# A new beginning of the first image and a new end of the last one, in a kernel that joins a Fourier neural operator and a 3x3 dilation

## The chip, the core and the metric

The kernel runs on one core of one Trainium2 chip. The metric is the device time of one execution in microseconds, and the median over several executions is what counts. Before the change it is 3658.42 us, the median of three executions that took 3650.33, 3659.02 and 3658.42 us.

A core has four compute engines that run side by side, each through its own list of instructions in order. TensorE (PE) multiplies matrices into an accumulator memory (PSUM); VectorE (DVE) does elementwise arithmetic, reductions, transposes and statistics; ScalarE (ACT) applies functions with a scale and a bias; GpSimd (POOL) is used here only to start transfers and for some constants. SyncE (SP) starts most transfers between the device's memory and the on-chip memory (SBUF). Engines wait for one another and for transfers through semaphores.

## The reference

The input x has 8 images of 8 channels of 256x256 pixels in float32. Two layers follow, each of them added to its own input.

```python
x = x + fno(gn(x))        # gn: mean and variance over each group of two channels
x = x + dilate(gn(x))     # 3x3 maximum, padded with -2

# fno, with 4 groups of 10 channels each
h = conv1x1([x, gridx, gridy], fc0)
for i in range(4):
    h = irfft2(modes_24x12(rfft2(h)) * sp_w[i]) + conv1x1(h, w_w[i])
    if i < 3: h = h * sigmoid(h * softplus(beta[i])) / 1.1
h = conv1x1(h, fc1)       # 10 to 128 channels in each group
h = h * sigmoid(h * softplus(beta[3])) / 1.1
return conv1x1(h, fc2)
```

The arithmetic on constants that matters here: softplus of the betas is multiplied into the weights (fc0 and w_w of layer 0, fc1), so that the activation becomes a plain Silu, and 1/(1.1 softplus) into the weights that follow. The group norm needs 1/sqrt(variance + eps).

## The kernel before

**Images and stages.** The eight images run one after another. For an image b, the four spectral layers run over eleven chunks of the state `h` (TensorE multiplies, ScalarE applies Silu, VectorE transposes for the next transform). After layer 3 the state goes to the device's memory, and the head (fc1, Silu, fc2, the sum with x, the dilation) of image b is worked off in small pieces between the steps of image b+1's layers. The order on TensorE, VectorE, ScalarE and SP is the order in which the program emits instructions (`tc.manual_schedule`); generators that `yield` let the main loop put pieces of one part between pieces of another.

**The beginning.** The program first emits loads: SP's queue gets the image (`load_x`, two halves of 1 MB, into `turned`), then `grp`, `fw`, `fw8`, `stack`, `er`, `unf`, `xe`, `wext` (lines 91 to 105), and GpSimd's queue the betas and the other constants. A transfer takes one of eight semaphores in turn, so the ninth transfer of a queue waits until the first has landed, the tenth for the second, and so on. Then come the constants' arithmetic: `softplus` (lines 139 to 153) for `beta_p` and `beta_a`, the factors `io`, the scaled fc1 and fc2 weights `w1` and `w2` (163 to 165), the products `p_wc` of fc0 and layer 0's weights on TensorE (171 to 175), `wc`, `wm`, `cv`, `cz` (176 to 198), and the scaled `wt` and `wext` (199 to 205). Lines 141 to 205 are emitted outside the hand-written order; in the profile they are found between the instructions of the first image's `start`.

**The first image.** `start(0, d)` (line 686) loads the first mode tables `t` and runs `spectrum_x`: eight `bn_stats` over the image (281), four `bn_aggr` (285), group means by TensorE (270, 272), variances, again group means, `rsqrt` (258), the normalisation of the image in four pieces (306), and then a chain of small transforms that alternates between TensorE (318, 324, 331, 343) and VectorE copies (319, 325, 334, 347). Products with `wext` (355) and a sum follow, then `mix` with the mode tables (420, 423), and `rows_even`, whose matmuls (496) and copies to `zt` (215, 217) precede the first burst of layer 0 (600, 606). For the later images the same generator is advanced inside the previous image's layer 3. Before the change, the main loop runs `start(0, d)` from end to end (941).

**rsqrt.** The start value comes from the integer form of the number, and four Newton steps of three dependent operations each follow (262 to 265). It is called once for each image's input and once for each image's output.

**The end of the last image.** Its output stays on chip in `ya` (16 rows of each of 128 stripes and one neighbour row above and below). Whenever two rows are complete, `add` calls `dilate_early(t)` (733): the maximum over three columns of these rows (`across`, into `ma`) and over three rows of those that have both neighbours (`down`, into `oa`). At t = 7 a transfer brings the last row of each stripe to row 0 of the next one (744). Then `dilate_last` runs `stats_end` (statistics of the image through two matmuls with `grp`, then `rsqrt`), finishes row 0 of the stripes (751 to 753), subtracts the mean and multiplies by 1/sigma (754), applies the padding values at the image's borders (756, 758), adds `ya` in four pieces of four rows (762) and sends each piece to the device's memory, from SP and GpSimd in turn (763).

Of the kernel before, what the change touches and what calls it, by code (L numbers as in the profile page):

```python
# [10 lines left out]
F32 = mybir.dt.float32  # L11
# [35 lines left out]
def fno_dilate_kernel(ctx: ExitStack, tc: tile.TileContext, a: dict, out: bass.AP):  # L47
# [14 lines left out]
    def ps_tri(name):  # L62
        return ps.tile([128, 3, 512], F32, tag="tri", bufs=2, name=name)
# [41 lines left out]
    nc.sync.dma_start(wext.rearrange("p g o j -> p (g o j)"), a["wext"].partition_broadcast(128))  # L105
# [30 lines left out]

    def softplus(t, n, name):
        e = const.tile([128, n], F32, tag=f"{name}_e", name=f"{name}_e")  # L140
        nc.vector.tensor_scalar(e, t, -1.0, None, ALU.mult)
        nc.vector.tensor_tensor(e, e, t, ALU.max)
        nc.scalar.activation(e, e, AF.Exp, scale=-1.0)
        nc.vector.tensor_scalar(e, e, 1.0, None, ALU.add)
        nc.scalar.activation(e, e, AF.Ln)
        sp = const.tile([128, n], F32, tag=f"{name}_sp", name=f"{name}_sp")
        nc.vector.tensor_scalar(sp, t, 0.0, None, ALU.max)
        nc.vector.tensor_tensor(sp, sp, e, ALU.add)
        nc.vector.tensor_scalar(sp, sp, 1e-20, None, ALU.max)
        rs = const.tile([128, n], F32, tag=f"{name}_rs", name=f"{name}_rs")  # L150
        nc.vector.tensor_scalar(rs, sp, 1.1, None, ALU.mult)
        nc.vector.reciprocal(rs, rs)
        return sp, rs

    sp_p, rs_p = softplus(beta_p, 4, "bp")
    sp_a, rs_a = softplus(beta_a, 4 * G, "ba")
    io = const.tile([128, 4 * G], F32, tag="io", name="io")
    nc.vector.tensor_copy(io[:, 0:4], sp_a[:, 0:4])  # L160
    nc.vector.tensor_tensor(io[:, 4:12], sp_a[:, 4:12], rs_a[:, 0:8], ALU.mult)
    nc.vector.tensor_copy(io[:, 12:16], rs_a[:, 8:12])
    nc.vector.tensor_scalar(w1, w1, sp_p[:, 3:4], None, ALU.mult)
    for g in range(G):
        nc.vector.tensor_scalar(w2[:, g, :], w2[:, g, :], rs_a[:, 12 + g : 13 + g], None, ALU.mult)


    wc = const.tile([128, 32], F32, tag="wc", name="wc")
    p = ps_tri("p_wc")
    for g in range(G):  # L170
        mm(p[32 * g : 32 * g + 6, 0, :32], fc0x[part(g), :], wt[part(g), 0, g, :], start=True, stop=True)
    for i in range(2):
        for r in range(4):
            mm(p[part(r), 1, NO * G * i : NO * G * (i + 1)], fc0c[:, i, :], wbd[:, NO * r : NO * (r + 1), :],
               start=True, stop=True)
    nc.vector.memset(wc, 0.0)
    for g in range(G):
        gs = slice(32 * g, 32 * g + 6)
        nc.vector.tensor_scalar(wc[gs, :], p[gs, 0, :32], sp_p[gs, 0:1], None, ALU.mult)

    wm = wbd
    nc.vector.memset(wm, 0.0)
    for g in range(G):
        nc.vector.tensor_scalar(wm[32 * g : 32 * g + 2, :WID, g], wc[32 * g : 32 * g + 2, :WID], -1.0, None, ALU.mult)
    cv = const.tile([128, 2, NO, G], F32, tag="cv", name="cv")
    nc.vector.tensor_tensor(
        cv.rearrange("p i o g -> p (i o) g"), p[:, 1, : 2 * NO * G].rearrange("p (i g) -> p i g", g=G),
        sp_a[:, 0:4].unsqueeze(1).to_broadcast([128, 2 * NO, G]), ALU.mult,
    )


    for i, l in enumerate((0, 2)):
        nc.vector.tensor_tensor(
            cz[:, i], cz[:, i], sp_a[:, 4 * l : 4 * l + 4].unsqueeze(1).to_broadcast([128, NO, G]), ALU.mult,
        )
    nc.vector.tensor_tensor(cz[:, 0], cz[:, 0], cv[:, 0], ALU.add)
    nc.vector.tensor_copy(cz[:, 2], cv[:, 1])
    nc.vector.tensor_scalar(cz1, cz1, sp_p[:, 1:2], None, ALU.mult)
    nc.vector.tensor_tensor(
        wt, wt, io.rearrange("p (l g) -> p l g", l=4).unsqueeze(3).to_broadcast([128, 4, G, 32]), ALU.mult,  # L200
    )
    nc.vector.tensor_tensor(
        wext.rearrange("p g o j -> p g (o j)"), wext.rearrange("p g o j -> p g (o j)"),
        io[:, 0:4].unsqueeze(2).to_broadcast([128, G, 5 * WID]), ALU.mult,
    )


    alone = [True]

# [523 lines left out]
    def dilate_early(t):  # L733

        across(1 + 2 * t, 3 + 2 * t)
        if t == 0:
            nc.gpsimd.dma_start(ya[0:127, 17, 1 : HW + 1], ya[1:128, 1, 1 : HW + 1])
        else:
            down(2 * t - 1, 2 * t + 1)
        if t == 3:  # L740
            nc.vector.tensor_scalar(ya[:, 17, :], ya[:, 17, :], edge[:, 1:2], None, ALU.min)
            across(17, 18)
        if t == 7:
            nc.gpsimd.dma_start(ya[1:128, 0, 1 : HW + 1], ya[0:127, 16, 1 : HW + 1])
            down(15, 16)

    def dilate_last(b, stats):
        d = {}
        yield from stats_end(stats, f"y{b}", d)
        mr = d["mr"]  # L750
        nc.vector.tensor_scalar(ya[:, 0, :], ya[:, 0, :], edge[:, 0:1], None, ALU.min)
        across(0, 1)
        down(0, 1)
        nc.vector.tensor_scalar(oa, oa, mr[:, 0:1], mr[:, 1:2], ALU.subtract, ALU.mult)
        for w in (0, HW - 1):
            nc.vector.tensor_scalar(oa[:, :, w : w + 1], oa[:, :, w : w + 1], PAD, None, ALU.max)
        for i, r in enumerate((0, 15)):
            nc.vector.tensor_scalar(oa[:, r, :], oa[:, r, :], edge[:, 2 + i : 3 + i], None, ALU.max)
        o_rows = out[b].rearrange("c (p r w) -> (c p) r w", p=16, r=16)
        for i in range(4):  # L760
            r = slice(4 * i, 4 * i + 4)
            nc.vector.tensor_tensor(oa[:, r], oa[:, r], ya[:, 4 * i + 1 : 4 * i + 5, 1 : HW + 1], ALU.add)
            (nc.sync, nc.gpsimd)[i % 2].dma_start(o_rows[:, r], oa[:, r])
        yield


# [22 lines left out]
    def head(b, stored, stats):  # L789
# [147 lines left out]

    stats_of = {}
    with tc.manual_schedule(engines={PE, DVE, ACT, SP}):
        d = {}  # L940
# [50 lines left out]
def _tables():  # L991
# [153 lines left out]
```

## Time and profile before

| what | value |
| --- | --- |
| median of three executions | 3658.42 us |
| the profiled execution | 3659.15 us |
| its span, from the first to the last instruction | 3657.4 us |
| TensorE busy | 3478.5 us, 95% |
| ScalarE busy | 2873.7 us, 79% |
| VectorE busy | 2381.7 us, 65% |
| first burst of layer 0 begins (L600) | 58.37 us |
| last add of the last image ends (L851) | 3631.87 us |
| last VectorE operation ends (L762) | 3651.53 us |

A line of the page or of an answer reads: line of the program, engine, operation, tile written<-tiles read, shape, count, and times. In a timeline the first two numbers are the start and the length in us, and square brackets give the idle time of the engine just before and what ended it. A view by waits gives who waited for whom: us in total, times, longest. "SPq" and "POOLq" are the queues of the engines that start transfers. The two spans of the program that the change touches are the first 60 us and the last 26 us; in the page's 40 slices of the span, TensorE is busy for nine tenths or more of each slice from the fifth to the last but one.

### The profile page before, as it was taken

The page shows a single profiled execution, that of the slowest core. Times are in us where ns is not written, and L with a number is a line of the kernel's source. Part 1 is how long each engine was busy: PE and PEld are TensorE (multiplying, and loading weights), DVE is VectorE, ACT ScalarE, POOL GpSimd, SP SyncE. Part 2 cuts the span into 40 slices and gives each one's busy share as a digit, 9 for nine tenths or more (in the row PEclk, how much of TensorE's full clock was granted, in tenths as well). Part 3 has the DMA queues.
Part 4 walks back from the last instruction along what each step waited for, and adds up shares of the span by engine and source line. Part 5 has one row for each costly group of instructions (what it writes and reads, how often), then busy time and mean ns, then how long its engine had stood idle before and what let it go on. Part 6 is the DMA issues. An engine that isn't in the chain of part 4 may idle for free.

```text
span 3657.4 us, 112630 instructions
## 1 busy us (share of the span) xinstructions
PE 3478.5 (95%) x50872; PEld 1271.2 (35%) x50872; DVE 2381.7 (65%) x3697; ACT 2873.7 (79%) x3035; POOL 117.0 (3%) x202
## 2 busy tenths in 40 slices
PE   5768999999999999999999999999999999999997
PEld 2323333333333333333333333333333333333222
DVE  6776656557775677756776577766777567772443
ACT  2435888888888888887888888888888888889986
POOL 1000000000000000000000000000000000000000
PEclk7878999999999999999999999999999999999998
DMA  3005211442225222271223512254222521225331
GB/s 93 16 15 206 58 47 50 152 121 65 76 87 185 81 60 73 87 226 55 64 60 126 183 56 76 64 166 119 67 76 87 192 81 53 71 70 191 83 84 48
DMA packets 114080, 344.70 MB, mean 94 GB/s; under 512 B 15985, under 2 KB 18481, under 8 KB 98177
## 3 DMA queue, kind: packets, MB, share of 16 engines
q1 hardware_dynamic: 95392, 276.32, 24.9%
q0 software_dynamic: 18208, 61.18, 5.3%
q8 instruction: 400, 6.55, 0.7%
q14 instruction: 80, 0.65, 0.1%
HBM read 213.44 MB, written 123.74 MB: 92 GB/s over the span
## 4 chain that ended last, share of the span: by engine, by line
PE 80%; DVE 13%; ACT 4%; issue 3%; DMA 0%; ACTq 0%; DVEq 0%; POOL 0%; POOLq 0%
PE p_fc L825 21%; PE p_fc L842 21%; PE p_z L606 10%; PE p_d L567 8%; PE p_z L603 8%; PE p_u L585 3%; PE p_z L600 3%; DVE y L851 2%; DVE S L423 2%; DVE turned L420 2%; DVE turned L550 2%; PE p_b L390 1%; DVE turned L381 1%; PE p_g L518 1%; ACT act L826 1%
## 5 line engine op out<-in xcount | busy, mean ns | idle before, releaser
L827 ACT ACTIVATE act<-p_fc 128x1536 f32<-128x1536 f32 x1024 | 1492.0, 1457 | 3.1 <-PE p_fc L825 3.1
L825 PE MATMUL p_fc<-hs,c_w 32*128 32x512 f32 x8192 | 1132.7, 625 | 24.6 <-DVE y L851 10.0
L842 PE MATMUL p_fc<-act,c_w 128*32 128x512 f32 x8192 | 1007.1, 599 | 0.5 <-ACT act L827 0.2
L826 ACT ACTIVATE act<-p_fc 128x512 f32<-128x512 f32 x1024 | 616.0, 602 | 199.7 <-PE p_fc L825 187.6
L550 DVE STREAM_TRANSPOSE turned<-h 128x1024 f32<-128x1024 f32 x528 | 632.6, 1226 | 196.0 <-ACT h L611 195.2
L611 ACT ACTIVATE h<-p_z 128x512 f32<-128x512 f32 (+1 forms) x528 | 512.0, 1021 | 205.8 <-PE p_z L606 205.8
L851 DVE TENSOR_TENSOR y<-p_fc,y 128x512 f32<-128x512 f32 x392 | 267.7, 683 | 526.0 <-PE p_fc L842 526.0
L825 PEld LDWEIGHTS p_fc<-hs,c_w 32*128 32x128 f32 x8192 | 357.9, 184 | 595.0 <-ACT act L826 260.2
L842 PEld LDWEIGHTS p_fc<-act,c_w 128*32 128x32 f32 x8192 | 222.4, 109 | 704.9 <-issue 327.4
L606 PE MATMUL p_z<-c_binv,zt 32*128 32x256 f32 x5632 | 414.2, 408 | 0.1
L606 PEld LDWEIGHTS p_z<-c_binv,zt 32*128 32x128 f32 x5632 | 261.2, 188 | 309.5 <-issue 296.1
L603 PE MATMUL p_z<-h,c_wt 32*32 32x512 f32 x8448 | 358.0, 601 | 7.9 <-ACT act L826 4.2
L567 PE MATMUL p_d<-turned,c_fw 32*32 32x480 f32 (+1 forms) x9216 | 308.0, 539 | 0.6 <-DVE turned L550 0.2
L575 ACT ACTIVATE turned<-p_d 128x1440 f32<-128x1440 f32 x144 | 183.1, 1272 | 89.7 <-PE p_d L567 86.6
L613 ACT ACTIVATE h<-p_z,c_bias 128x512 f32<-128x512 f32 (+1 forms) x176 | 186.6, 1111 | 72.0 <-PE p_z L606 71.8
L215 ACT ACTIVATE zt<-p_g 128x198 f32<-128x198 f32 (+2 forms) x132 | 62.5, 583 | 177.6 <-PE p_g L496 93.7
L423 DVE TENSOR_REDUCE S<-turned 128x80 f32<-128x800 f32 x192 | 188.9, 984 | 5.9
L420 DVE TENSOR_TENSOR turned<-t,B 128x800 f32<-128x800 f32 x192 | 188.7, 983 | 1.1
L567 PEld LDWEIGHTS p_d<-turned,c_fw 32*32 32x32 f32 x9216 | 127.5, 103 | 165.5 <-issue 63.8
L381 DVE STREAM_TRANSPOSE turned<-zt 128x960 f32<-128x960 f32 x96 | 177.1, 1868 | 2.5
L603 PEld LDWEIGHTS p_z<-h,c_wt 32*32 32x32 f32 x8448 | 92.9, 103 | 175.5 <-DVE y L851 48.8
L585 PE MATMUL p_u<-turned,c_stack 128*32 128x480 f32 (+1 forms) x1152 | 136.7, 543 | 7.2 <-DVE turned L574 6.2
(198 smaller groups left out, 1748.2 us busy)
## 6 DMA issues: line engine op xcount, KB each, us to landing
stored<-h SPq DMA_DIRECT2D x88, 1024.0 KB
hs<-stored SPq DMA_DIRECT2D x352, 256.0 KB
t<-in_spw SPq DMA_DIRECT2D x96, 400.0 KB
yin<-y_rows POOLq DMA_DIRECT2D x56, 512.0 KB, 5.1
h<-in_xp SPq DMA_DIRECT2D x352, 48.0 KB
turned<-in_xw SPq DMA_DIRECT2D x16, 1024.0 KB
y<-in_x SPq DMA_DIRECT2D x56, 256.0 KB
y_rows<-y POOLq DMA_DIRECT2D x56, 256.0 KB, 3.9
```

The lines of the kernel that those rows point to most:

```text
L420: nc.vector.tensor_tensor(pr, sw[k], bt[:, k2, k].unsqueeze(2).to_broadcast([128, G, 2 * WID, WID]), ALU.mult)
L423: nc.vector.tensor_reduce(s[k2][:, k].rearrange("p s o g -> p (s o) g"), pr.rearrange("p g m i -> p m g i"), AX.X, ALU.add,)
L550: nc.vector.transpose(dst[:, 2 * i : 2 * i + 2], h[:, c, 2 * i : 2 * i + 2].rearrange("p f (s x) -> p f s x", s=2))
L567: mm(banks[q][part(v % 4), : 240 * n], fw8[part(q), v, :], t[part(q), :, :, v, : NBLK * WID], start=v < 4, stop=v >= 4)
L603: mm(o, wt[part(q), l, g, :], h[part(q), c, f, :], start=True, stop=False)
L606: mm(banks[q][:, HW * s : HW * (s + 1)], zt[part(q), 2 * c + s].rearrange("p f o -> p (f o)"), binv[part(q), :], start=False, stop=s == 1)
L611: nc.scalar.activation(dst, src, AF.Silu)
L825: mm(banks[g], w1[part(g), blk, :], hs[k][part(g), :], start=True, stop=True)
L826: nc.scalar.activation(act[:, 0, :], one, AF.Silu)
L827: nc.scalar.activation(act[:, 1:4, :], tri, AF.Silu)
L842: mm(acc[part(g), :], w2[:, g, 15 - rb - i : 47 - rb - i], act[:, g, :], start=i == 0, stop=i == 1)
L851: nc.vector.tensor_tensor(y, sums, y, ALU.add)
```

## The change

It has five parts.

1. SP's loads are put in another order: `er`, `fw`, `unf`, `xe` and `wext` follow the image, and `fw8`, `stack` and `grp` come last.
2. The arithmetic on the constants becomes a generator, `prepare()`, in eight pieces. The main loop emits a piece after the third, sixth, eighth, tenth, twelfth, fourteenth and sixteenth yield of `start(0, d)`, and the last piece after it.
3. `rsqrt` makes three Newton steps instead of four, for every image.
4. At the last image's t = 7 only the transfer of the neighbour rows is started; `dilate_early(7)` is no longer called, and `dilate_last` does its work itself.
5. `dilate_last` is rewritten. The statistics come first; the remaining `across` operations lie between their two matmuls. ScalarE takes the mean off `oa`, piece by piece (`centre`). The padding values are scaled by sigma instead of the rows by 1/sigma (`ends`), and one operation multiplies by 1/sigma and adds `ya`. Five pieces (rows 4 to 7, 8 to 11, 12 to 15, 0 and 1, 2 and 3) go out, all from SP. In the `edge` table the value for rows that are no border becomes -1e30, so that its product with sigma stays finite.

```diff
     ident = const.tile([128, 128], F32, tag="ident", name="ident")
     make_identity(nc, ident)
-    grp = load("grp", (128, 128), nc.sync)
-    fw = load("fw", (128, 2, 32), nc.sync)
-    fw8 = load("fw8", (128, 8, 32), nc.sync)
-    stack = load("stack", (128, 32), nc.sync)
...
     er = load("er", (128, 2, 32), nc.sync)
+    fw = load("fw", (128, 2, 32), nc.sync)
     unf = load("unf", (128, 3, 32), nc.sync)
...
     nc.sync.dma_start(wext.rearrange("p g o j -> p (g o j)"), a["wext"].partition_broadcast(128))
+    fw8 = load("fw8", (128, 8, 32), nc.sync)
+    stack = load("stack", (128, 32), nc.sync)
+    grp = load("grp", (128, 128), nc.sync)
...
+    def prepare():
...
+        for i, (t, _, _) in enumerate(pair):
+            nc.vector.tensor_scalar(e[i], t, -1.0, None, ALU.mult)
+            nc.vector.tensor_tensor(e[i], e[i], t, ALU.max)
+        for i in range(2):
+            nc.scalar.activation(e[i], e[i], AF.Exp, scale=-1.0)
+        yield
+        for i, (t, _, _) in enumerate(pair):
+            nc.vector.tensor_scalar(e[i], e[i], 1.0, None, ALU.add)
+            nc.vector.tensor_scalar(sp[i], t, 0.0, None, ALU.max)
+        for i in range(2):
+            nc.scalar.activation(e[i], e[i], AF.Ln)
+        yield
+        p = ps_tri("p_wc")
...
+        yield
+        for i in range(2):
+            nc.vector.tensor_tensor(sp[i], sp[i], e[i], ALU.add)
+            nc.vector.tensor_scalar(sp[i], sp[i], 1e-20, None, ALU.max)
+            nc.vector.tensor_scalar(rs[i], sp[i], 1.1, None, ALU.mult)
+            nc.vector.reciprocal(rs[i], rs[i])
...
+        yield
+        nc.vector.memset(wc, 0.0)
...
+        yield
+        nc.vector.tensor_tensor(
+            wt, wt, io.rearrange("p (l g) -> p l g", l=4).unsqueeze(3).to_broadcast([128, 4, G, 32]), ALU.mult,
+        )
+        nc.vector.tensor_scalar(w1, w1, sp_p[:, 3:4], None, ALU.mult)
+        for g in range(G):
+            nc.vector.tensor_scalar(w2[:, g, :], w2[:, g, :], rs_a[:, 12 + g : 13 + g], None, ALU.mult)
+        yield
...
-        for _ in range(4):
+        for _ in range(3):
...
-        if t == 7:
-            nc.gpsimd.dma_start(ya[1:128, 0, 1 : HW + 1], ya[0:127, 16, 1 : HW + 1])
-            down(15, 16)
 
     def dilate_last(b, stats):
...
+        nc.vector.bn_aggr(mv, stats.rearrange("p n s -> p (n s)"))
+        p = ps_tri("p_st_end")[:, 0, 0:1]
+        mm(p, grp, mv[:, 0:1], start=True, stop=True)
+        rows = ma[:, 15:17]
+        nc.vector.tensor_tensor(rows, ya[:, 15:17, 0:HW], ya[:, 15:17, 1 : HW + 1], ALU.max)
+        nc.vector.tensor_copy(m, p)
+        nc.vector.tensor_tensor(d, mv[:, 0:1], m, ALU.subtract)
+        nc.vector.scalar_tensor_tensor(mv[:, 1:2], d, d, mv[:, 1:2], ALU.mult, ALU.add)
+        q = ps_tri("p_sv_end")[:, 0, 0:1]
+        mm(q, grp, mv[:, 1:2], start=True, stop=True)
+        nc.vector.tensor_scalar(less, m, -1.0, None, ALU.mult)
+        nc.vector.tensor_tensor(rows, rows, ya[:, 15:17, 2 : HW + 2], ALU.max)
+        v = mv[:, 1:2]
+        nc.vector.tensor_scalar(v, q, EPS, None, ALU.add)
+        rsqrt(v, r, d)
+        nc.vector.tensor_tensor(d, v, r, ALU.mult)
+        nc.vector.tensor_scalar(ends[:, 1:2], d, -2.0 * PAD, None, ALU.mult)
+        nc.vector.tensor_scalar(ends[:, 2:4], edge[:, 2:4], d, -2.0, ALU.mult, ALU.mult)
+
+        def centre(r0, r1):
+            nc.scalar.activation(oa[:, r0:r1], oa[:, r0:r1], AF.Identity, bias=less)
+
+        centre(4, 8)
+        centre(8, 12)
+        centre(1, 4)
+        centre(12, 13)
+        down(13, 15)
+        centre(13, 15)
+        down(15, 16)
+        centre(15, 16)
         nc.vector.tensor_scalar(ya[:, 0, :], ya[:, 0, :], edge[:, 0:1], None, ALU.min)
         across(0, 1)
         down(0, 1)
-        nc.vector.tensor_scalar(oa, oa, mr[:, 0:1], mr[:, 1:2], ALU.subtract, ALU.mult)
...
+        centre(0, 1)
         o_rows = out[b].rearrange("c (p r w) -> (c p) r w", p=16, r=16)
-        for i in range(4):
-            r = slice(4 * i, 4 * i + 4)
-            nc.vector.tensor_tensor(oa[:, r], oa[:, r], ya[:, 4 * i + 1 : 4 * i + 5, 1 : HW + 1], ALU.add)
-            (nc.sync, nc.gpsimd)[i % 2].dma_start(o_rows[:, r], oa[:, r])
+        for r0, r1 in ((4, 8), (8, 12), (12, 16), (0, 2), (2, 4)):
+            o = oa[:, r0:r1]
+            side = o[:, :, 0 : HW : HW - 1]
+            nc.vector.tensor_scalar(side, side, ends[:, 1:2], None, ALU.max)
+            for i, row in enumerate((0, 15)):
+                if r0 <= row < r1:
+                    nc.vector.tensor_scalar(oa[:, row, :], oa[:, row, :], ends[:, 2 + i : 3 + i], None, ALU.max)
+            nc.vector.scalar_tensor_tensor(o, o, r, ya[:, r0 + 1 : r1 + 1, 1 : HW + 1], ALU.mult, ALU.add)
+            nc.sync.dma_start(o_rows[:, r0:r1], o)
         yield
...
-                dilate_early(t)
+                if t < 7:
+                    dilate_early(t)
+                else:
+                    nc.gpsimd.dma_start(ya[1:128, 0, 1 : HW + 1], ya[0:127, 16, 1 : HW + 1])
...
-        d = {}
-        for _ in start(0, d):
-            pass
+        d, ready = {}, prepare()
+        for n, _ in enumerate(start(0, d), 1):
+            if n in (3, 6, 8, 10, 12, 14, 16):
+                next(ready)
+        next(ready)
...
-    edge[:, 2], edge[:, 3] = np.where(top, PAD, -BIG), np.where(bottom, PAD, -BIG)
+    edge[:, 2], edge[:, 3] = np.where(top, PAD, -1e30), np.where(bottom, PAD, -1e30)
```

The pieces of `prepare()` that the cut leaves out are the same operations as before: the twelve `p_wc` matmuls, `io` and the scaled `wext` behind the reciprocals, the four `wc` operations, `cv` with the memset and the four operations of `wm`, and `cz`. As built, the order on VectorE begins with the eight `bn_stats` and the four `bn_aggr`; on TensorE the `p_wc` matmuls stay between the second group means and L318; `wt`, `w1` and `w2` come between the last operation on `fz` and the first `zt` copy.

More of the change, by code (lines that the diff above doesn't have):

```diff
@@ L135, in fno_dilate_kernel @@
     nc.vector.memset(dc, 0.0)
[L139 to L153, printed above, removed]
@@ L157, in fno_dilate_kernel @@
-    sp_p, rs_p = softplus(beta_p, 4, "bp")
-    sp_a, rs_a = softplus(beta_a, 4 * G, "ba")
-    io = const.tile([128, 4 * G], F32, tag="io", name="io")
[L160 to L165, printed above, removed]
@@ L168, in fno_dilate_kernel @@
-    wc = const.tile([128, 32], F32, tag="wc", name="wc")
[L169 to L179, printed above, removed]
+    io = const.tile([128, 4 * G], F32, tag="io", name="io")
@@ L181, in fno_dilate_kernel @@
+    wc = const.tile([128, 32], F32, tag="wc", name="wc")
     wm = wbd
-    nc.vector.memset(wm, 0.0)
-    for g in range(G):
-        nc.vector.tensor_scalar(wm[32 * g : 32 * g + 2, :WID, g], wc[32 * g : 32 * g + 2, :WID], -1.0, None, ALU.mult)
     cv = const.tile([128, 2, NO, G], F32, tag="cv", name="cv")
[L186 to L189, printed above, removed]
@@ L192, in fno_dilate_kernel @@
-    for i, l in enumerate((0, 2)):
+    def prepare():
+        pair = ((beta_p, 4, "bp"), (beta_a, 4 * G, "ba"))
+        e, sp, rs = [[const.tile([128, n], F32, tag=f"{name}_{k}", name=f"{name}_{k}") for _, n, name in pair]
+                     for k in ("e", "sp", "rs")]
+        for i, (t, _, _) in enumerate(pair):
[12 more added lines that the diff above has]
+        for g in range(G):
+            mm(p[32 * g : 32 * g + 6, 0, :32], fc0x[part(g), :], wt[part(g), 0, g, :], start=True, stop=True)
+        for i in range(2):
+            for r in range(4):
+                mm(p[part(r), 1, NO * G * i : NO * G * (i + 1)], fc0c[:, i, :], wbd[:, NO * r : NO * (r + 1), :],
+                   start=True, stop=True)
+        yield
+        for i in range(2):
+            nc.vector.tensor_tensor(sp[i], sp[i], e[i], ALU.add)
+            nc.vector.tensor_scalar(sp[i], sp[i], 1e-20, None, ALU.max)
+            nc.vector.tensor_scalar(rs[i], sp[i], 1.1, None, ALU.mult)
+            nc.vector.reciprocal(rs[i], rs[i])
+        (sp_p, sp_a), (_, rs_a) = sp, rs
+        nc.vector.tensor_copy(io[:, 0:4], sp_a[:, 0:4])
+        nc.vector.tensor_tensor(io[:, 4:12], sp_a[:, 4:12], rs_a[:, 0:8], ALU.mult)
+        nc.vector.tensor_copy(io[:, 12:16], rs_a[:, 8:12])
@@ L193, in fno_dilate_kernel @@
         nc.vector.tensor_tensor(
-            cz[:, i], cz[:, i], sp_a[:, 4 * l : 4 * l + 4].unsqueeze(1).to_broadcast([128, NO, G]), ALU.mult,
-        )
[L196 to L205, printed above, removed]
+            wext.rearrange("p g o j -> p g (o j)"), wext.rearrange("p g o j -> p g (o j)"),
@@ new lines, in prepare @@
+            io[:, 0:4].unsqueeze(2).to_broadcast([128, G, 5 * WID]), ALU.mult,
+        )
+        yield
+        nc.vector.memset(wc, 0.0)
+        for g in range(G):
+            gs = slice(32 * g, 32 * g + 6)
+            nc.vector.tensor_scalar(wc[gs, :], p[gs, 0, :32], sp_p[gs, 0:1], None, ALU.mult)
+        yield
+        nc.vector.tensor_tensor(
+            cv.rearrange("p i o g -> p (i o) g"), p[:, 1, : 2 * NO * G].rearrange("p (i g) -> p i g", g=G),
+            sp_a[:, 0:4].unsqueeze(1).to_broadcast([128, 2 * NO, G]), ALU.mult,
+        )
@@ new lines, in prepare @@
+        nc.vector.memset(wm, 0.0)
+        for g in range(G):
+            gs = slice(32 * g, 32 * g + 2)
+            nc.vector.tensor_scalar(wm[gs, :WID, g], wc[gs, :WID], -1.0, None, ALU.mult)
+        yield
+        for i, l in enumerate((0, 2)):
+            nc.vector.tensor_tensor(
+                cz[:, i], cz[:, i], sp_a[:, 4 * l : 4 * l + 4].unsqueeze(1).to_broadcast([128, NO, G]), ALU.mult,
+            )
+        nc.vector.tensor_tensor(cz[:, 0], cz[:, 0], cv[:, 0], ALU.add)
+        nc.vector.tensor_copy(cz[:, 2], cv[:, 1])
@@ L208, in fno_dilate_kernel @@
+        nc.vector.tensor_scalar(cz1, cz1, sp_p[:, 1:2], None, ALU.mult)
+        yield
+        nc.vector.tensor_tensor(
+            wt, wt, io.rearrange("p (l g) -> p l g", l=4).unsqueeze(3).to_broadcast([128, 4, G, 32]), ALU.mult,
+        )
+        nc.vector.tensor_scalar(w1, w1, sp_p[:, 3:4], None, ALU.mult)
+        for g in range(G):
+            nc.vector.tensor_scalar(w2[:, g, :], w2[:, g, :], rs_a[:, 12 + g : 13 + g], None, ALU.mult)
+        yield
     alone = [True]
@@ L742, in dilate_early @@
             across(17, 18)
-        if t == 7:
-            nc.gpsimd.dma_start(ya[1:128, 0, 1 : HW + 1], ya[0:127, 16, 1 : HW + 1])
-            down(15, 16)
     def dilate_last(b, stats):
-        d = {}
-        yield from stats_end(stats, f"y{b}", d)
-        mr = d["mr"]
+        mv = sb.tile([128, 2], F32, tag="mv", name="mv_end")
+        mr = sb.tile([128, 2], F32, tag="mr", bufs=4, name="mr_end")
+        d = sb.tile([128, 1], F32, tag="d", name="d_end")
+        ends = sb.tile([128, 4], F32, tag="mv", name="ends")
+        m, r, less = mr[:, 0:1], mr[:, 1:2], ends[:, 0:1]
+        nc.vector.bn_aggr(mv, stats.rearrange("p n s -> p (n s)"))
[26 more added lines that the diff above has]
+        centre(15, 16)
         nc.vector.tensor_scalar(ya[:, 0, :], ya[:, 0, :], edge[:, 0:1], None, ALU.min)
@@ L753, in dilate_last @@
         down(0, 1)
[L754 to L758, printed above, removed]
-        o_rows = out[b].rearrange("c (p r w) -> (c p) r w", p=16, r=16)
-        for i in range(4):
-            r = slice(4 * i, 4 * i + 4)
-            nc.vector.tensor_tensor(oa[:, r], oa[:, r], ya[:, 4 * i + 1 : 4 * i + 5, 1 : HW + 1], ALU.add)
-            (nc.sync, nc.gpsimd)[i % 2].dma_start(o_rows[:, r], oa[:, r])
+        centre(0, 1)
+        o_rows = out[b].rearrange("c (p r w) -> (c p) r w", p=16, r=16)
+        for r0, r1 in ((4, 8), (8, 12), (12, 16), (0, 2), (2, 4)):
[7 more added lines that the diff above has]
+            nc.sync.dma_start(o_rows[:, r0:r1], o)
         yield
@@ L939, in fno_dilate_kernel @@
     with tc.manual_schedule(engines={PE, DVE, ACT, SP}):
-        d = {}
-        for _ in start(0, d):
-            pass
+        d, ready = {}, prepare()
[3 more added lines that the diff above has]
+        next(ready)
         for b in range(n_img):
```

## The prediction

> **What bounds the kernel now.** I read the page first, then the waits of the first 60 us, then the timeline of both ends, since the change touches only these and one helper (rsqrt).
>
> ```profile
> PE 3478.5 (95%) x50872; PEld 1271.2 (35%) x50872; DVE 2381.7 (65%) x3697; ACT 2873.7 (79%) x3035; POOL 117.0 (3%) x202
> PE 80%; DVE 13%; ACT 4%; issue 3%; DMA 0%; ACTq 0%; DVEq 0%; POOL 0%; POOLq 0%
> ```
>
> Over the span TensorE carries the chain that ended last (80%). That average hides both ends: before 58 us and after 3632 us TensorE works for a few us at a time, and VectorE, in program order, sets the pace. What stood in front of VectorE at the start is in the waits of 0 to 60 us (one for VectorE, one for SP's queue):
>
> ```profile
> DVE bp_e L141 <- DMA c_beta_p<-in_beta_p: 3.9, 1, 3.9
> SPq L105 <- DMA turned<-in_xw: 4.1, 1, 4.1
> ```
>
> VectorE waits first for the betas, then for softplus, although the image is there: SP's wait at L105 is for the image's second half, and the timeline has the next issue at 10.17, so that half landed by then; the same reading of the issue at 5.69 puts the first half at about 5.6. In the timeline, VectorE's statistics come only after that arithmetic:
>
> ```profile
> 10.17 0.33 SPq L105 DMA_DIRECT2D c_wext<-in_wext  x1
> 14.26 2.46 DVE L281 BATCH_NORM_STATS2 bn_x<-turned 128x6 f32<-128x512 f32 x4
> 16.64 0.41 DVE L285 BATCH_NORM_AGGREGATE mv_x<-bn_x 128x2 f32<-128x12 f32 x4
> 19.66 0.17 DVE L302 TENSOR_SCALAR d_x<-p_sv_x 128x5 f32<-128x5 f32 x1 [0.93 <-PE p_sv_x L272]
> 26.37 2.98 DVE L306 TENSOR_SCALAR turned<-turned,mr_x 128x1024 f32<-128x1024 f32 x4
> ```
>
> Everything after 26.37 up to the first row matmuls (54.67) hangs on this line. At the end, TensorE's last add is over at 3631.87, and then VectorE alone runs to 3651.53:
>
> ```profile
> 3636.14 0.58 DVE L231 BATCH_NORM_AGGREGATE mv_y<-h 128x2 f32<-128x96 f32 x1
> 3641.40 0.35 DVE L751 TENSOR_SCALAR h<-h,c_edge 128x258 f32<-128x258 f32 x1
> 3643.62 2.41 DVE L754 TENSOR_SCALAR h<-h,mr_y 128x4096 f32<-128x4096 f32 x1
> 3646.90 4.62 DVE L762 TENSOR_TENSOR h<-h 128x1024 f32<-128x1024 f32 x4
> ```
>
> The view by windows has the output's data until 3655.0 (near 400 GB/s, 1.3 us per 512 KB) and nothing more to the span's end at 3657.4: a tail of 2.4 us.
>
> **The start, step by step.** (1) The statistics move in front of everything that needs the betas. First four: 5.7 to 8.2, free. Second four: from 10.2, 2.46 as above; the aggregates add 0.41 less 0.08 overlap: they end at 13.0, not 17.05: **4.1 earlier**. (2) From there to L302 is 2.61 (17.05 to 19.66), two round trips to TensorE with 0.93 idle each. The betas' eight small operations (0.17, pitch 0.1 to 0.2) go into these two waits, about 0.6 and 0.45: cost 0. Exp, Ln and their table load (1.28) end on ScalarE by about 15.7, and the results are asked for at about 20.8. The twelve p_wc matmuls lie between two uses of TensorE (0.7 of over 2 us). L302 falls at 15.6. (3) L302 to L306 took 6.71, because wext, wt, wc, wm, cv, cz, w1 and w2 were mixed in. Image 1 shows it bare: L302 at 305.24, L306 at 308.11, 2.87 with four Newton steps; a step is three dependent operations, 0.20 apart. Three steps: 2.27. L306 begins at 17.9, **8.5 earlier**. (4) What was mixed in is paid later, in VectorE's waits: softplus' rest, io, wext and the memset (13 operations, about 2.4 from their pitches) in 2.60 idle before L319: 0. wc (0.09 and 1.02) in 0.81 before L325: +0.35. cv, wm (1.0) in 1.16 before L334: 0. cz (0.65) in 0.62 before L347: +0.05. wt, w1, w2 (0.68, 0.41, 0.70) in 1.42 before the first zt copy L217: +0.37, which the first bursts inherit since TensorE waits for zt at 60.3. Start: 8.5 - 0.77 = **7.7**.
>
> The reordered SP loads: er, fw, unf, xe, wext, fw8 (400 KB) now follow the image instead of 380 KB, and wext no longer waits; the mode tables t start some 0.7 us sooner and h's 44 loads behind them too. grp, now last before t, is first needed by image 0's output statistics. Nothing waits that did not. If the image's second half landed later by d, d is lost; I take 0, and 0 to 3 as ends, 3 being about what 1.2 MB of t would take.
>
> **The Newton step in images 1 to 7** (x and y, 0.6 each): 0. After L306's first piece VectorE idles anyway (near 1147: 0.99 until TensorE's p_fc); after the y chain at 816.5 it idles 0.80 for ScalarE. At image 1 the fourth L306 piece paces one matmul of L318 by perhaps 0.1. Ends: 0 to -1.
>
> **The end.** From 3631.87: bn_stats to 3632.67. The aggregate comes at once, to 3633.27, instead of after L725 to L731 (3.5). TensorE's answer 0.68 later, the chain L239 to L252 1.35: 3635.3. Two across operations (0.69 each) fit into those two waits (0.68, 0.74): +0.1. rsqrt with three steps 2.73 - 0.58 = 2.15, three new small ones 0.5: 3638.0. Then what was moved behind: down(13,15) 1.43, down(15,16) 0.86, and row 0 as before (L751 to L731, 2.2): 3642.5, against 3643.62. The real gain follows: L754 (2.41) leaves VectorE. ScalarE takes the mean off rows 1 to 12 from 3634.6: by L613, an Identity with a pointer bias (688 ns at 512, 1533 at 1536), pieces of 1024, 1024, 768, 256 cost 1.11, 1.11, 0.90, 0.48, done at 3638.2; rows 13 to 15 and 0 follow each down. The last ends near 3643 and is asked for at 3647; cover 4 us. Five side maxima (0.17, 0.19 with their wait) 0.95, two edge rows 0.62, and 4096 elements of a three-operand operation.
>
> That one has no row at this size. [...] L754 (0.59 ns an element) beside L762 (1.19) shows it, so fusing multiply and add makes nothing faster than L762; only moving the subtraction to ScalarE pays. Next rows: L762 1.216 (1.13 pitch) per 1024; L849, this operation from PSUM at 512, 747 against 693. Ends 1.13 and 1.31; I take 1.2, and 0.67 for 512: 4.94 in all (-0.3, +0.5).
>
> VectorE ends at 3642.5 + 6.5 = 3649.0. Pieces are ready at 3643.9, 3645.3, 3647.0, 3648.15, 3649.0; SP's first transfer before took 0.8 from issue (3648.14) to data. The data never queue more than 0.2: the last 256 KB run 3649.8 to 3650.45; plus 2.4: 3652.85 against 3657.4: **4.55**. All issues now sit on SP, which has nothing else left; POOL's two go.
>
> **Sum.** 7.7 + 4.55 = 12.25. The profiled execution is 3659.15 (span 3657.4), so 3646.9; the median of the runs shown is 0.7 lower: **3646**, 0.34% down.
>
> **The clock.** TensorE is slow in the first image:
>
> ```profile
> 58.00:62.00 4.00, 4.00 (x51) 1.53 (x48) 0.67 (x1) 2.42 (x3) 0.00 (x0) 0.50 0.02 4
> 70.00:74.00 4.00, 4.00 (x52) 1.54 (x48) 2.37 (x3) 1.94 (x2) 0.00 (x0) 0.50 0.00 0
> 76.00:78.00 2.00, 2.00 (x64) 0.88 (x61) 0.86 (x2) 1.21 (x2) 0.00 (x0) 1.00 0.00 0
> ```
>
> (window; us, busy of PE, PEld, DVE, ACT, POOL; clock; DMA.) [...] busy all of 58 to 74 at 0.50, and full only a good microsecond into the first transform (74.33). [...] by the row the slow stretch moves along with the work and costs what it did. I take the row. [...]
>
> **Rivals.** *The clock rises early* in the first image: 3646 - 5.4 = 3640.5. For it: one of the three runs was at 3650.33, 8 under the others. Against: this profile. *The start gives less*: the image's half lands up to 3 later or the small operations overrun their waits by 1 to 2: 3649 to 3650. For it: eight extra waits on ScalarE, TensorE and loads in that stretch, two covers with under 0.2 to spare; against: every result is ready microseconds early. *The change moves nothing at the start* (the image, not the betas, was late): only the end, 3654; against: the issue at 10.17. *Slower*: moved by 7.7, the first transforms do not lift the clock, and layer 0 of image 0 goes on at 0.50. In 78 to 107 TensorE is busy some 28 us; at half clock that costs up to 25: 3671. It decides once the slow stretch lasts some 25 us longer than now. For it: 16 busy us did not lift it; against: transforms lifted it within 1.2 us.
>
> **How the numbers follow.** Forecast (3643 to 3649) 0.60; early clock 0.14; less start 0.19; end only 0.04; slower 0.03. The range 3638 to 3652 takes in the first three, the unknown ends and part of the runs' spread. 0.3%, about what a measurement of this kernel can tell from none, is 11 us: 3647.4. Three quarters of the forecast case, the early clock and little of the third are under it: 0.64 faster; slower 0.03; same 0.33.
>
> **What would show it.** In the new trace: the second statistics at about 10.2, L306's line at about 18, the first row matmuls near 47; aggregate near 0.8 us after the last add, ScalarE idle before row 0's piece, last VectorE operation 17.1 after the last add, tail 2.4. Wrong would be: idle time for a DMA before the second statistics, waits of TensorE for the constants, the three-operand operation over 1.3, or a first full clock elsewhere than at the first transform.

## The result, and the profile after

The changed kernel takes 3642.47 us, the median of five executions (3640.12 to 3646.95); the kernel before, run beside it, 3659.02 (3650.33 to 3661.19). The ratio is 0.996, with a 95% interval of 0.9949 to 0.9972. The forecast was 3646, a gain of 12.25; the medians are 16.55 apart, the spans of the two profiled executions (3657.4 and 3640.6) 16.8.

Shares and chain in the page of the changed kernel have hardly moved:

```profile
PE 3475.6 (95%) x50872; PEld 1269.6 (35%) x50872; DVE 2374.1 (65%) x3656; ACT 2878.2 (79%) x3042; POOL 115.9 (3%) x200
PE 79%; DVE 13%; ACT 4%; issue 3%; DMA 1%; SPq 0%; DVEq 0%; ACTq 0%
```

VectorE has 41 operations less, TensorE as many as before. The timeline of the changed kernel's start (start, length, engine, line, operation, tiles) answers to the lines from 14.26 on:

```profile
10.00 2.47 DVE L286 BATCH_NORM_STATS2 bn_x<-turned 128x6 f32<-128x512 f32 x4 [1.86 <-DMA turned<-in_xw]
12.39 0.41 DVE L290 BATCH_NORM_AGGREGATE mv_x<-bn_x 128x2 f32<-128x12 f32 x4
15.41 0.16 DVE L307 TENSOR_SCALAR d_x<-p_sv_x 128x5 f32<-128x5 f32 x1 [0.63 <-PE p_sv_x L277]
17.68 2.98 DVE L311 TENSOR_SCALAR turned<-turned,mr_x 128x1024 f32<-128x1024 f32 x4
```

The statistics now wait for the image, and the normalisation (L311, was L306) begins 8.69 earlier. The end, from the aggregate to ScalarE's work, the first fused operation and the last:

```profile
3621.10 0.59 DVE L756 BATCH_NORM_AGGREGATE mv_end<-h 128x2 f32<-128x96 f32 x1
3622.87 3.41 ACT L776 ACTIVATE h<-h,ends 128x1024 f32<-128x1024 f32 x4 [4.46 <-DVE ends L766]
3630.58 1.29 DVE L798 SCALAR_TENSOR_TENSOR h<-h,mr_end 128x1024 f32<-128x1024 f32 x1
3636.68 0.75 DVE L798 SCALAR_TENSOR_TENSOR h<-h,mr_end 128x512 f32<-128x512 f32 x1
```

From the start of the last add (3631.18 before, 3619.59 after) to the end of the span it is 21.01 us instead of 26.17: 5.2 gained. That leaves 11.6 at the last add. The starts of the same instructions in both traces, before less after, say where they arose:

| instruction, time before | gain |
| --- | --- |
| first row matmuls, 54.67 | 8.6 |
| image 1, variance (L302), 305.24 | 6.2 |
| image 1, add at 343.2 | 7.1 |
| image 2, add at 784.1, then at 794.8 | 7.16, then 8.70 |
| image 3, adds at 1217.6 and 1228.2 | 8.73, then 10.26 |
| image 4, adds at 1651.1 and 1661.7 | 10.36, then 11.89 |
| image 5, adds at 2084.5 and 2095.1 | 11.78, then 13.31 |
| images 6 and 7, to 3495.5 | 13.2 to 13.3 |
| adds at 3505.8 and 3631.2 | 11.6 |

Four jumps of 1.53 in images 2 to 5 and a step back of 1.66 near 3500 make 4.5 us, in a stretch of the program where the two kernels differ by one Newton step only. The view by windows, cut at the jump of image 2, has the reason. First the kernel before, then the changed one at the same place and in image 6 (window; us, busy of PE, PEld, DVE, ACT, POOL; clock; DMA):

```profile
785.42:788.84 3.42, 3.42 (x83) 1.37 (x80) 0.20 (x2) 2.89 (x6) 0.00 (x0) 1.00 0.02 5
788.84:792.25 3.41, 3.41 (x39) 1.92 (x24) 2.10 (x2) 1.90 (x3) 0.00 (x0) 0.50 0.01 2
```

```profile
779.49:782.90 3.41, 3.41 (x81) 1.82 (x65) 0.00 (x0) 2.88 (x3) 0.00 (x0) 1.00 0.02 7
2506.64:2510.05 3.41, 3.41 (x84) 1.38 (x86) 0.00 (x0) 2.88 (x4) 0.00 (x0) 1.00 0.02 5
2510.05:2513.46 3.41, 3.41 (x24) 1.71 (x24) 2.37 (x2) 2.35 (x3) 0.00 (x0) 0.50 0.01 2
```

TensorE is busy throughout, and yet for 3.41 us its clock is 0.50. Over its whole trace, the kernel before has such a half-clock window at the opening of layer 0 in each of images 2 to 7, six in all; the changed kernel in images 6 and 7 only, and one more at 3489.7, after 2.15 us in which TensorE waits for an add (it is busy for 1.27 of the 3.42 us before that window). Image 0 and the very end apart, nothing else in either trace is slow. In one trace all rises and falls of the clock, those of image 0 too, lie on one grid of 3.413 us: at 0.36 us past a multiple of it before, 1.25 after. A piece of this grid is called a window below; where the text only counts windows, those at half clock are meant.

### The profile page after: what moved, and what is told of

It reads as the page before. It is cut to its first block, busy times and chain, and to the rows that moved or that the text cites. A ratio compares the mean times of both kernels' runs of the same rounds, so it can differ in the third digit from the quotient of the medians.

```text
span 3640.6 us, 112595 instructions
## 1 busy us (share of the span) xinstructions
PE 3475.6 (95%) x50872; PEld 1269.6 (35%) x50872; DVE 2374.1 (65%) x3656; ACT 2878.2 (79%) x3042; POOL 115.9 (3%) x200
## 4 chain that ended last, share of the span: by engine, by line
PE 79%; DVE 13%; ACT 4%; issue 3%; DMA 1%; SPq 0%; DVEq 0%; ACTq 0%
PE p_fc L861 21%; PE p_fc L878 21%; PE p_z L611 10%; PE p_d L572 8%; PE p_z L608 8%; PE p_u L590 3%; PE p_z L605 3%; DVE y L887 2%; DVE S L428 2%; DVE turned L425 2%; DVE turned L555 2%; DVE turned L386 1%; PE p_g L523 1%; PE p_b L395 1%; ACT act L862 1%
```

## The experiments

Theory A: the change took some 12.3 us of work away, and the other 4.5 are a difference in half-clock windows, dealt out anew in each execution by the grid's phase (where its lines fall in the program). Theory B: the Newton step is worth 1.5 us in each of images 2 to 5. Rivals C (a changed order costs something of its own), D (the program's timing fixes the windows) and E (the clock follows TensorE's busy time, not how many rows its matmuls take) came up on the way.

**The step alone.** Only `range(4)` becomes `range(3)` in the kernel before.

> The kernel before with three Newton steps in rsqrt instead of four, nothing else. Theory A (work plus clock windows): of the 16.8 us between the two profiles, about 12.3 is work that left (start 7, end 5.2), and 4.5 is the difference in half-clock windows of 3.41 us that fall at the start of layer 0 in images 2 to 7 (six in the profile of before, two there and one more near 3490 in that of after; 1.55 us each). The step itself then saves 0.6 in image 1 and 0.6 at the end, 1.2 in all: 3658.0 with the same six windows, 3648.7 with none, and any jump of the shift against before, image by image, is 1.55 and stands exactly where one of the two profiles shows a clock of 0.50. Theory B (the step is worth some 1.5 us in each of images 2 to 5, through the waits of the statistics): 3653 to 3654 with six windows too, the shift grows by 1.5 in images 2, 3, 4 and 5 whatever the clock shows.

Median 3653.89 (13 executions, 3650.43 to 3659.1), before 3656.82 (19), ratio 0.9993 (0.9985 to 1.0001). The profiled execution (3653.89) has windows in images 6 and 7 and at 3496. Against the trace of before the shift goes from -0.7 before image 1 to +0.55 in it, then jumps by 1.44 to 1.58 in images 2, 3, 4 and 5, where before alone has a window, and by nothing in 6 and 7, where both have one. B's jumps are there, but in this trace both theories foretell them. The next run parts them.

**All but the step.**

```diff
-        for _ in range(3):
+        for _ in range(4):
```

> The changed kernel with four Newton steps in rsqrt, nothing else undone. Theory A: 1.2 us more work than the changed kernel: 3639.0 plus 1.55 for each half-clock window in images 2 to 7 (0 to 6 of them, as the windows happen to lie), so 3639 to 3648, and the shift against before jumps by 1.55 only where the two profiles differ in a window. Theory B: the 4.5 us of images 2 to 5 are missing: 3647 to 3648, with a shift against before that stays at 6 to 7 from image 1 to image 7 whatever the clock shows.

Median 3648.86 (7 executions, 3640.28 to 3652.08). In the profile (3649.23) the windows lie in images 4 to 7, at 3495.6, at 328.1 (still in image 0's layer 3) and at image 1's opening, and so the shift against before falls by 1.5 in image 1 (5.82 to 4.28), rises by 1.2 in image 2 and 1.5 in image 3, and then stays at 6.8 to 7.1 up to image 7. With four Newton steps in both kernels the jumps are still there, where the clock differs: B is out.

**Beginning alone, end alone, and the changed kernel once more.**

> The kernel before with the new beginning alone (order of SP's loads, the constants' arithmetic in pieces), four Newton steps, old end. The first four runs bear out windows of 3.41 us on a grid whose phase differs from execution to execution; taking off 1.55 us for each half-clock window of images 1 to 7 (1.66 for the one near 3490), the profiled executions come to 3649.9 before, 3649.1 with the step alone, 3638.2 with all but the step, 3637.7 after. Theory A: the beginning is worth 7 us of work (6 to 8): the profiled time less its windows is 3642 to 3644. Rival D (part of the windows is the beginning's own doing, because it moves everything by a fixed amount): the profile shows the windows where that of after shows them, images 6 and 7 only.

> The kernel before with the new end alone (including the transfer of the neighbour row at t = 7 and the table of the edges), four Newton steps. Theory A: from the start of the last add to the end of the span 26.2 becomes 21.6 (21.0 as after, and 0.6 for the fourth step): 4.6 us; the profiled time less its windows is 3645.3 (3644.5 to 3646). Rival D: windows in images 2 to 7 as in the profile of before, all six, since nothing ahead of 3630 differs.

> The changed kernel once more, unaltered, for a second profile and more executions. Theory A: the half-clock windows of images 2 to 7 lie on another phase of the 3.41 us grid, so another number of them (0 to 6) falls into the openings of layer 0; the profiled time less its windows is again 3637.7 (1 us either way for the first image), single executions spread over 3637 to 3649. Rival D (the program's own timing fixes the windows): again images 6 and 7 and the one near 3490, and 3642 to 3643.

The beginning alone: median 3642.98 (5, 3641.44 to 3653.36); its profiled execution (3642.51) has no window after image 0 at all. The end alone: median 3653.76 (16, 3644.55 to 3659.94); 21.58 us from the last add to the end of the span, as expected, with six windows (which D foretold as well) and a seventh at 3504.6. The changed kernel again: 3643.87 (5, 3637.69 to 3646.66). Its profile is of the same program as the trace above, and the windows lie elsewhere, on a phase of 0.73 instead of 1.25:

```profile
775.55:778.97 3.42, 3.42 (x82) 1.25 (x80) 0.00 (x0) 2.89 (x5) 0.00 (x0) 1.00 0.02 5
778.97:782.38 3.41, 3.41 (x27) 1.91 (x24) 2.37 (x2) 2.22 (x3) 0.00 (x0) 0.50 0.01 2
```

Six windows at the openings, images 2 to 7, where its other profile has two, and in both one near 3490: D is out, the phase is the execution's own. At 1.55 a window, and 1.66 for the one near 3490, the profiled executions less their windows are 3649.9 before, 3637.7 and 3634.5 after, 3649.1 with the step alone, 3639.8 with all but the step (the two at 328.1 and in image 1 cost 1.5 together, not 1.55 each as an expectation had them), 3642.5 and 3647.2 with beginning and end alone. The last is 2 above its expectation: its first bursts began 1.35 later than in the profile of before, part of the scatter of the first 60 us (below). And 3634.5 is 3.2 below what was expected of the same program's second profile: the windows of image 0 are not taken off, and there the number differs too (25 behind 100 us before and after, 24 in this profile, 23 with the beginning alone).

**What sets a window off.** At the opening two bursts follow each other, each 32 matmuls of 6 rows and 16 of 32. The kernel before, and the changed one at the same place:

```profile
785.51 1.57 PE L600 MATMUL p_z<-h,wcn 6*32 6x512 f32 x32
787.02 1.15 PE L606 MATMUL p_z<-c_binv,zt 32*128 32x256 f32 x16
788.09 1.50 PE L600 MATMUL p_z<-h,wcn 6*32 6x512 f32 x32
789.52 2.09 PE L606 MATMUL p_z<-c_binv,zt 32*128 32x256 f32 x16
```

```profile
778.35 1.57 PE L605 MATMUL p_z<-h,wcn 6*32 6x512 f32 x32
779.86 1.15 PE L611 MATMUL p_z<-c_binv,zt 32*128 32x256 f32 x16
780.93 1.18 PE L605 MATMUL p_z<-h,wcn 6*32 6x512 f32 x32
782.05 1.15 PE L611 MATMUL p_z<-c_binv,zt 32*128 32x256 f32 x16
```

In the window up to 788.84 the 6-row matmuls have 1.50 (785.51 to 787.02) and 0.75 us: 66%. In 779.49 to 782.90 they have 0.37 and 1.12: 44%, and the clock stays. Over the openings of images 1 to 7 in the seven profiles with 6 rows and the old order, every window that they filled to 63 to 69% was followed by a slow one (27 times), and none that they filled to 62% or less.

Two attempts put head work between the bursts, so that their 6-row matmuls fill less of any one window, first fc2 alone in all three layers, then fc2 and fc1 in layer 0 only:

```diff
-                yield "t"
+                yield "ct"
                 burst(1)
...
-                yield "cf"
+                yield "f"
```

```diff
-                yield "t"
+                yield "cft" if l == 0 else "t"
                 burst(1)
...
-                yield "cf"
+                yield None if l == 0 else "cf"
```

> The kernel before, where the main loop emits the 128-row matmuls of the head (fc2, L842) between the first two bursts of a layer instead of after them, from image 1 on; the same work. Theory A: [...] no half-clock window in layer 0 of images 2 to 7, and the time is 3659.15 - 6 x 1.55 = 3649.9 (3648.5 to 3651.5) in every execution, which then differ by under 2 us. Theory B (the windows cost nothing, what differs is the order of work): 3658 to 3660. Rival C (the head's matmuls between the bursts delay ScalarE or VectorE): no windows but 1 us or more lost in each of seven images, 3657 or more.

> The changed kernel with the same split of the first two bursts. Theory A: 3642.47 - 2 x 1.55 = 3639.4 if the window near 3490 is still there, 3637.8 if not; 3636.5 to 3640 in every execution, and 12 us (11 to 13.5) under the kernel before with the split: that difference is the change without the windows. Theory B: 3641 to 3643, 16.8 under the split kernel before. Rival C: 3645 or more.

> The changed kernel where, in layer 0 of images 1 to 7 only, both kinds of the head's matmuls (fc2, then fc1) are emitted between the first two bursts. The earlier split put fc2 alone there, in three layers of seven images, and left ScalarE idle for 0.5 and 2.1 us each time. Theory A with ScalarE fed: no half-clock window in these openings and 3637 to 3640 in every execution, a spread of under 3 us. Rival C (ScalarE still comes late, 1.65 us for each of seven openings as in the first split): no windows, but 3648 to 3651.

They took 3694.63, 3677.93 and 3650.63: C each time. ScalarE's Silu sets the pace there, and the first split leaves it without work between its bursts (view of ScalarE in the second kernel; idle time and what ended it in brackets):

```profile
785.36 1.94 ACT L616 ACTIVATE h<-p_z 128x512 f32<-128x512 f32 x2 [0.53 <-PE p_z L611]
789.38 1.94 ACT L616 ACTIVATE h<-p_z 128x512 f32<-128x512 f32 x2 [2.08 <-PE p_z L611]
```

The windows didn't all go either (two to four in each of these profiles; all but one near 3500 are at or behind the openings, some after a share of 54%, which other times had no such effect). Order was the wrong lever; rows are a free one, if the few rows of these matmuls are what the slow windows come from. The 6-row matmuls may as well take all 32 rows of a stripe, since `wcn` is zero in the other 26 and their contents are finite from image 1 on:

```diff
-                        k = slice(32 * q, 32 * q + 6)
+                        k = slice(32 * q, 32 * q + (6 if b == 0 else 32))
```

> The kernel before, where from image 1 on the burst's first matmuls take 32 rows of each stripe instead of 6: the 26 more rows meet weights that are zero, so the sums and the number of columns, the instructions and their order stay. Only how much of the array works changes. Theory A, sharpened [...]: no half-clock window at the openings of layer 0 in images 2 to 7, and 3649.9 (3647 to 3652, with the spread of the first image and 1.66 for the window near 3490) in place of 3657 to 3658. Theory E [...]: the windows stay, their number as the phase has it, and the mean stays near 3657.

> The changed kernel with the same 32 rows from image 1 on. Theory A: no half-clock window at the openings of layer 0, 3634.5 to 3637.7 from the two profiles of the changed kernel less their windows, 1.66 more where the one near 3490 falls: median near 3637, and 12 us (10.5 to 13.5) under the kernel before with 32 rows: that is the change without its luck with the clock. Theory E: 3640 to 3646 as the changed kernel.

Before with 32 rows: 3650.82 (16 executions, 3648.43 to 3653.63; ratio to before 0.9982, 0.9975 to 0.9990). Changed with 32 rows: 3638.61 (5, 3635.26 to 3640.21; 0.9947, 0.9935 to 0.9960). Neither profile has a window at an opening of images 1 to 7, and not because the grid fell well. In the kernel before with 32 rows the same two bursts, as long as with 6 rows, fill 69% of a window (TensorE's lines, then the view by windows):

```profile
784.88 1.57 PE L600 MATMUL p_z<-h,wcn 32*32 32x512 f32 x32
787.47 1.18 PE L600 MATMUL p_z<-h,wcn 32*32 32x512 f32 x32
```

```profile
785.03:788.44 3.41, 3.41 (x80) 1.24 (x78) 0.00 (x0) 2.88 (x5) 0.00 (x0) 1.00 0.02 5
788.44:791.86 3.42, 3.42 (x52) 1.63 (x40) 2.34 (x2) 3.17 (x4) 0.00 (x0) 1.00 0.01 2
```

The clock stays at 1.00, where behind 66% with 6 rows it was 0.50. E is out. The two kernels are **12.2** apart in their medians (12.5 in their means): that is the change without the windows at the openings. It is not free of all luck: the profile of the changed one still has a window at 3487.05, image 0 has 6 rows as before, and five executions with a standard deviation of 2.0 leave their mean uncertain by some 0.9.

**Image 0 as well.**

```diff
+    for c in range(NCH):
+        nc.gpsimd.memset(h[:, c], 0.0)
...
-                        k = slice(32 * q, 32 * q + 6)
+                        k = slice(32 * q, 32 * q + 32)
```

> The changed kernel with 32 rows in image 0 too; for that GpSimd first sets the state h to zero, in eleven operations at the very beginning, each ahead of the load of its chunk. If the 6 rows are also what keeps TensorE at 0.50 during the first bursts of image 0 (four bursts of about 4.0 us each, 2.2 at full clock), the clock comes up within a window or so of the bursts' start instead of in the first transform: 3 to 5 us less than with 32 rows from image 1 on, so near 3633. If not, the same 3637. If GpSimd's memsets hold up VectorE's statistics or the loads of h, more than 3637, and the second statistics begin later than 10.0.

3651.38 (17): slower. The statistics came in time (9.87), the operation behind them did not (VectorE, then GpSimd):

```profile
12.59 19.91 DVE L152 TENSOR_SCALAR bp_e<-c_beta_p 128x4 f32<-128x4 f32 x1
...
13.18 19.28 POOL L120 MEMSET h<- 128x2048 f32 x11
```

One operation on 128x4 elements took 19.91 us instead of 0.11: it ended at 32.50, GpSimd's eleventh memset at 32.46. But the clock came up 4.2 us after the first bursts' start (70.28, full at 74.47), where with 6 rows it took 19.3 (51.02, full at 70.31). So the zeros went to ScalarE, which is idle then, and for four chunks only:

```diff
+    for c in range(4):
+        for f in range(0, NQ, 2):
+            nc.scalar.activation(h[:, c, f : f + 2].rearrange("p f w -> p (f w)"),
+                                 yin.rearrange("p r w -> p (r w)")[:, : 2 * PIX], AF.Identity, scale=0.0)
...
-                        k = slice(32 * q, 32 * q + 6)
+                        k = slice(32 * q, 32 * q + (6 if b == 0 and c > 3 else 32))
```

> The changed kernel with 32 rows from image 1 on and for the first four chunks of image 0. ScalarE, idle there until 13, sets these four chunks of h to zero in eight operations of 1024 from about 2 to 11, ahead of their loads. With GpSimd's memset the first bursts started 19.3 late and the first fold 15.1 late against 32 rows from image 1 on, so the early clock is worth 4.2; without the wait on GpSimd it should remain: the clock full within 3.5 us of the first bursts, the second statistics at 10.0 as before, and a median 3 to 5 under the 3638.6 of 32 rows from image 1 on: 3634.5 (3633.5 to 3636). If Exp comes late behind ScalarE's zeros, softplus is late at 20.6 and the time is 3636 to 3639. [...]

**3633.13** (5, 3628.86 to 3633.84; ratio to before 0.9929, 0.9915 to 0.9942), the fastest of all; before, run beside it, 3658.01. From its timeline, ScalarE's zeros and TensorE's first bursts:

```profile
2.12 7.68 ACT L136 ACTIVATE h<-yin 128x1024 f32<-128x1024 f32 x8
```

```profile
51.30 2.01 PE L609 MATMUL p_z<-h,wcn 32*32 32x512 f32 x32
53.24 1.40 PE L615 MATMUL p_z<-c_binv,zt 32*128 32x256 f32 x16
54.57 1.19 PE L609 MATMUL p_z<-h,wcn 32*32 32x512 f32 x32
```

The zeros are done at 9.80, ahead of Exp (13.04). The clock is full at 53.79, and the second burst takes 2.2 us instead of 4.0.

## Why the prediction was right, point by point

- **The sum.** 12.25 was forecast; with the windows at the openings excluded 12.2 is measured. The direction and the range held; 3642.47 lies 0.5 below the case held likeliest (3643 to 3649). The further 4.3 of the 16.55 match the 4.5 of windows by which the two profiles differ; the other executions' windows are not known. That forecast and measurement agree to a tenth is luck: the parts below, as far as they can be had one by one (7.6, 0.6 and 5.2), come to 13.4, the first of them with a scatter of about 1.
- **The step that failed** is what was said of the clock: "the slow stretch moves along with the work and costs what it did". For the images behind the first no term was set, that is, nothing. The page's row of clocks has nines behind the first image, and windows of 3.41 us don't show in slices of 91 us. Six of them, 9.3 us, stood in the trace of before, and weren't looked for. In image 0 the step held only roughly: from the first burst to the full clock it is 17.1 us before (58.37 to 75.45) and 19.8 after (49.75 to 69.52). The clock's edges there came 5.9 earlier, not 8.6, and the gain falls from 7.6 at the first burst's second half to 6.2 at image 1. These 1.4 are about what 2.7 us more at half clock cost (a burst takes 4.0 us there, 2.2 at the full clock); the prediction counted nothing for them.
- **The slow rows.** The prediction took the slow rows of 58 to 74 as they stood. Its rival "the clock rises early" (5.4 less, by the author's estimate: three of the four bursts at 2.2 us instead of 4.0) didn't occur here. Busy time alone does not bring the full clock: TensorE was busy throughout the windows ahead of the slow ones at the openings (3.42 of 3.42 us in 785.42 to 788.84), and 32 rows instead of 6, with nothing else changed on TensorE, keep the clock up there (1.00 for 0.50), and in image 0 raise it (2.5 us after the first bursts' start, 51.30 to 53.79, where with 6 rows it took 19.3). So rows bring about what the rival had, and gain 5.5 (3638.61 to 3633.13, medians of five executions each). By what means they do it was not shown.
- **The start**, 7.7. L306's line at 17.9: measured 17.68. In this pair of traces the gain falls from 9.01 at the end of L318's sixteen matmuls to 8.63 at the first row matmuls, as the losses of wc and cz (0.40) would have it. That of wt, w1, w2 (0.37) didn't come: it is still 8.62 at the first burst. The first burst's second half (`binv`) begins at 60.8 on average in the five traces with the old beginning, at 52.8 in the six with the new one and three steps: 8.0. At image 1's variance it is 7.6 (305.95 and 298.35, five traces each, with 6 rows in image 0), though the pair in the table has 6.2.
- **The scatter of the first 60 us** comes mostly from the clock. L318's matmuls took 4.8 to 6.1 us in five traces of the old beginning, 4.3 to 5.7 in eight of the new. A trace's first record of the clock is its rise to full (31.08 before, 21.73 after); ahead of it four of these matmuls begin every 0.85 us, behind it every 0.43. Half the time ahead of the rise plus the time behind it is 2.9 in twelve of the thirteen (in the other, 3.2, a piece of the image came 0.6 late). So the grid's phase sets the length. (Views by windows print 1.00 where the trace has no record.) In the changed kernel's trace another 1.0 us was lost inside the first burst, with no wait that the profile shows; this stays open.
- **The Newton step**, 0.6 in image 0 (in the start) and "0 (ends 0 to -1)" in images 1 to 7: mis-sized in image 1. There 0.6 is gained at L306 and kept (L318's stretch goes from 3.26 to 2.67); this is inside the ends, but not the 0.1 that the prediction saw there. In images 2 to 7 it is 0, as said: the 0.6 gained at L306 (7.15 to 7.75 at 710.8) is gone at its second piece (7.15 at 714.4).
- **The end**, 4.55: measured 5.2 (21.01 for 26.17). VectorE's last operation ended 17.1 us after the last add's end, as forecast. The three-operand operation took 1.28 and 0.75, not 1.2 and 0.67, inside its ends: 1.25 ns an element with two tensors, as L762's add before (1.19), where L754 with one took 0.59. The tail was mis-sized: from VectorE's last operation (3637.43) to the end of the span (3640.6) 3.2, not 3.85. Of it the stretch behind the output's last data took 1.5 us (3639.1 to 3640.6), 1.5 with the end alone too, where the prediction took 2.4 from the kernel before; the cause stays open.
- **Chances.** 3642.47 is under the bound of 3647.4 that made it "faster". The rival "slower" found no sign: the clock rises within the first transform as before (66.71 to 70.12; full at 69.52). One sign of being wrong did come, idle time for a DMA before the second statistics (1.86 in the line at 10.00). It contradicted the prediction's own sum, which had VectorE free from 8.2 and the image's second half there at 10.2.

What stays open: whether the changed kernel also meets fewer windows on average. Over all executions here the mean is 3657.1 before (89) and 3642.6 after (10), 14.5 apart and so 2.0 more than the 12.5 with 32 rows; with standard deviations of 3.4 and 3.2, the mean of ten is uncertain by 1.0 of itself, and that may be chance.

## What to carry to other kernels

When two traces are compared, tabulate the shift of the same instruction along the whole run, and look at the clock wherever it jumps; here a step of 1.5 us that came back once per image was not work. Try to pad matmuls of few rows with zero weights where the data are finite: here it cost TensorE nothing (1.57 us for a burst's 32 matmuls, with 6 rows as with 32), and kept its clock (1.00 at the openings, where 6 rows had windows at 0.50). Judge a change of some us in such a kernel by variants that are free of the clock's luck, or by many executions.

## What the runs showed of the hardware that was not expected

- **The windows lock on.** An image without one takes 431.9 us (778.35 to 1210.24 in the openings of the changed kernel), which moves the grid by 1.6 us from image to image; one with a window takes 433.49, which is 127 times 3.413. So the first image that is hit has all later ones hit at the same place: in the six profiled executions with 6 rows and the old order that were hit in image 2 or later, every later image was hit too. One hit in image 1 (all but the step) did not hold: images 2 and 3 went free, with shares of 60 and 44%.
- **VectorE behind GpSimd.** In the run with the memsets one VectorE operation on 128x4 elements took 19.91 us (12.59 to 32.50), 0.11 in the changed kernel, and ended 0.04 after the last of GpSimd's eleven memsets (13.18 to 32.46). That the memsets held it is argued from this coincidence; no run tests it, and by what means they would was not shown.
- Executions of the kernel before with 32 rows from image 1 on scatter less: 1.4 us (standard deviation, 16 executions) against 3.4 with 6 rows (89).
